# Per-head softmax weights through DRAM instead of through TensorE in an attention stage of a fused two-layer kernel

## The chip, the cores and the metric

The kernel runs on one core of a Trainium2 chip. The metric is the device time of one execution in microseconds. The time before the change is the median of 3 runs.

## The reference

Two layers work on an image of 2 x 768 x 64 x 64 in 32-bit floats, both with a group norm before and a residual behind. The first is a Mamba-like scan layer; the change does not touch it. The second, which matters here, is an attention without pairs of tokens. In short, for each batch, with 4096 tokens n, 768 channels in 12 heads h of 64 channels d:

```python
w      = (x3 @ W_qkv.T)                                   # (h, n, d)
norm   = sqrt(sum_n w*w)                                   # per channel
logits = sum_d (w / norm)**2 * temp                        # (h, n)
Pi     = softmax(logits, axis=heads)                       # (h, n)
Pi_n   = Pi / (sum_n Pi + 1e-8)
dots   = sum_n Pi_n * w**2                                 # (h, d)
out    = -(w * Pi) / (1 + dots)
out    = out @ W_out.T
```

Pi has one number for each head and token. It must be multiplied with w, which lies with channels on the partitions; so each of the 12 rows of Pi has to be copied to the 64 partitions of its head.

## The kernel before

Each batch is cut into 8 tiles of 512 tokens (`NQ`, `QL`), and the 768 channels into 6 chunks of 128 (`KM`); a chunk holds two heads. The product with W_qkv ("p1") and the product with W_out ("p3") of a tile are made of 6 products of 128 output channels each. Most of them run in `strassen`, a schedule that saves matmuls and that fills TensorE. Between these schedules lies `attention(b, ...)`, once for each batch. It makes Pi for all 8 tiles of batch b, multiplies it with w, and sums `dots`.

The order of all instructions is written out by hand (the schedule is manual); each engine, and SP's queue of loads and stores, takes its own instructions in that order. Waits between engines come from the data.

So that TensorE has something to do in `attention`, 12 ordinary products are held back for it: for batch 0 the p1 products of the first two tiles of batch 1, for batch 1 the p3 products of the last two tiles of batch 0. `product()` runs one of them; `half_a()` runs its first three matmuls and issues the loads of a product three places on, `half_b(between)` the last three, then whatever is passed as `between`, then the eviction (on ScalarE for p1, on VectorE for p3, which is stored by SP).

For one tile j the steps are:

- `squares`: ScalarE squares w, six chunks, two tiles ahead.
- `head_rows`: TensorE sums the squares over the channels of each head (pr); ScalarE copies the result (lt).
- `head_columns`: TensorE turns it so that tokens lie on partitions (pl).
- `softmax_a`: VectorE takes the maximum over the heads (mx) and subtracts it (e), ScalarE takes exp. pr and pl share one bank of PSUM.
- `softmax_b`: VectorE normalizes e, copies it four times side by side into `pi4`, and sums it into `phs`; TensorE transposes the copy (pt), ScalarE copies the result to `pit`.
- `spread`: six matmuls with a matrix of zeros and ones, `esel`, copy each row of `pit` to the 64 partitions of its head, into PSUM (ppz, ppo).
- `times_pi`: VectorE multiplies this with w into a fresh slot v; w is kept for the next step.
- `pi_sums`: VectorE multiplies v with w and sums over the tokens in one instruction, into `dots`; the slot of w is given back.

In the loop over j, step j runs `spread`, `times_pi` and `pi_sums` of tile j beside `head_rows`, `head_columns` and the softmax of tile j + 1. Ahead of the loop stand two products (one of them the argument `lead`) and the softmax of tile 0. Behind it come one product, the sum over tokens of Pi (a matmul into pp), the factor `at` = -1 / (1 + dots), the first loads and sums of the next `strassen` (`behind()`), and one more product (`more`).

Slots of 128 x 512 floats are handed out by `take()` and given back by `give()`; they are reused in the order in which they came back. `wk` is a pool of work tiles with two buffers for each tag unless a number is given.

Of the kernel before, what the change touches and what calls it, by code (L numbers as in the profile page):

```python
# [7 lines left out]
F32 = mybir.dt.float32  # L8
# [59 lines left out]
def both_layers(  # L68
    ctx, tc, nc, consts, x, in_wP, xp_wP, dt_wP, out_wT, pc_in, comb_in, pick_in, xsum_in, gavg_in, gsel_in, wo_dr, bc_dr, s_dr, x1, stats1,
    qkvP, woutP, temp_c, hcol_in, hsel_in, esel_in, out  # L70
# [583 lines left out]
    x1s, w1s, pis, pits, ats, dots, phs = {}, {}, {}, {}, {}, {}, {}  # L654
# [371 lines left out]
    def head_rows(b, j):  # L1026
# [6 lines left out]
        lt = wk.tile([P, QL], F32, tag="du", name=f"lt{b}_{j}", bufs=2)  # L1033
# [20 lines left out]
    def softmax_b(b, j):  # L1054
# [5 lines left out]
        pi = pi4[j % 2]  # L1060
        nc.vector.tensor_copy(pi[:, :, :, :HEADS], e.unsqueeze(2).to_broadcast([P, NB4, 4, HEADS]))
# [3 lines left out]
        for q in range(NB4):  # L1065
            nc.tensor.matmul(  # L1066
                pt[:, q * P : (q + 1) * P], pi[:, q, :, :].rearrange("p c h -> p (c h)"), ident, start=True, stop=True
            )
        pit = wk.tile([P, QL], F32, tag="delta", name=f"pit{b}_{j}", bufs=3)
        nc.scalar.copy(pit, pt)  # L1070
        pits[b, j] = pit

    def spread(b, j, ms):

        for m in ms:
            if m in (0, 4):
                pits["z"] = psZ.tile([P, 2, 512], F32, tag="pz", name=f"ppz{b}_{j}_{m}")
            if m == 2:
                pits["o"] = [psO.tile([P, 512], F32, tag=f"po{e}", name=f"ppo{e}_{b}_{j}") for e in range(2)]
            pb = pits["o"][m % 2] if m in (2, 3) else pits["z"][:, m % 2, :]  # L1080
            r = 32 * (m % 4)
            nc.tensor.matmul(pb, esel[r : r + HEADS, m, :], pits[b, j][r : r + HEADS, :], start=True, stop=True)  # L1082
            pits[b, j, m] = pb

    def times_pi(b, j, ms):
        for m in ms:
            w, v = w1s[b, m, j], take()
            nc.vector.tensor_mul(v, pits.pop((b, j, m)), w)
            w1s[b, m, j] = v
            pis[b, j, m] = w  # L1090

    def pi_sums(b, j, ms):
        for m in ms:
            w = pis.pop((b, j, m))
            nc.vector.tensor_tensor_reduce(w, w1s[b, m, j], w, 1.0, 0.0, ALU.mult, ALU.add, dots[b][:, m, j : j + 1])
            give(w)

    def attention(b, lead, more, behind):
# [4 lines left out]
        product(lead)  # L1103
        head_rows(b, 0)
        squares(b, 1)
        half_a()
        head_columns(b, 0)
        softmax_a(b, 0)
        half_b(lambda: softmax_b(b, 0))
        for j in range(NQ):  # L1110
            last = j + 1 == NQ
            if not last:
                head_rows(b, j + 1)
            spread(b, j, range(4))
            times_pi(b, j, range(4))
# [497 lines left out]
```

## Time and profile before

| | us |
|---|---|
| median of 3 runs | 3725.79 (3723.79 to 3728.96) |
| profiled execution | 3722.47 |
| its span, first to last instruction | 3720.7 |
| first `attention`, first product to the next Strassen schedule | 2939.2 to 3051.1 |
| second `attention` | 3385.4 to 3498.6 |
| PE busy in the span | 3532.7 (95%) |
| DVE (VectorE) busy | 2871.3 (77%) |
| ACT (ScalarE) busy | 2559.3 (69%) |
| POOL (GpSimd) busy | 1779.2 (48%) |

The mean granted clock of TensorE was 0.987. The table's shares are means over the whole span, most of which is the first layer; what the change is worth is read from the two stretches of `attention`. PE is TensorE's matmuls, PEld its loads of weights. A line of the profile names the line of the kernel, the engine, the operation and the tiles (out<-in). A matmul of 32-bit floats appears as two instructions. Where the profile lists "u" and "v", these are slots.

### The profile page before, as it was taken

The page shows a single profiled execution, that of the slowest core. Times are in us where ns is not written, and L with a number is a line of the kernel's source. Part 1 is how long each engine was busy: PE and PEld are TensorE (multiplying, and loading weights), DVE is VectorE, ACT ScalarE, POOL GpSimd, SP SyncE. Part 2 cuts the span into 40 slices and gives each one's busy share as a digit, 9 for nine tenths or more (in the row PEclk, how much of TensorE's full clock was granted, in tenths as well). Part 3 has the DMA queues.
Part 4 walks back from the last instruction along what each step waited for, and adds up shares of the span by engine and source line. Part 5 has one row for each costly group of instructions (what it writes and reads, how often), then busy time and mean ns, then how long its engine had stood idle before and what let it go on. Part 6 is the DMA issues. An engine that isn't in the chain of part 4 may idle for free. (4 is left out here: it accounts for less than half of the span.)

```text
span 3720.7 us, 37791 instructions
## 1 busy us (share of the span) xinstructions
PE 3532.7 (95%) x11088; PEld 1756.0 (47%) x11088; DVE 2871.3 (77%) x2615; ACT 2559.3 (69%) x4982; POOL 1779.2 (48%) x1813
## 2 busy tenths in 40 slices
PE   5968999999999999999899999999999999999999
PEld 3423333333333333333343333333347658886688
DVE  7899999999999999999999999997721362224522
ACT  2688889888988898889788888897633542244221
POOL 0355555555555555555555655554443313330232
PEclk9978999999999999999999999999999999999999
DMA  9877898998989999898898989897676538764487
GB/s 352 234 171 161 181 206 181 207 205 189 209 175 211 199 199 207 183 205 181 189 206 193 208 175 208 198 201 181 139 206 176 194 92 267 253 210 124 155 270 245
DMA packets 380302, 738.98 MB, mean 199 GB/s; under 512 B 44305, under 2 KB 116945, under 8 KB 376001
## 3 DMA queue, kind: packets, MB, share of 16 engines
q0 software_dynamic: 146208, 270.08, 42.8%
q1 hardware_dynamic: 233888, 466.49, 38.2%
q8 instruction: 90, 1.47, 0.2%
q14 instruction: 116, 0.94, 0.1%
HBM read 440.96 MB, written 60.03 MB: 135 GB/s over the span
## 5 line engine op out<-in xcount | busy, mean ns | idle before, releaser
L362 PE MATMUL pa<-u,w 128*128 128x512 f32 (+1 forms) x2304 | 1045.2, 604 | 31.3 <-ACT carry L377 19.5
L603 PE MATMUL po<-u,w 128*128 128x512 f32 x2256 | 1019.1, 602 | 44.8 <-DVE u L615 44.5
L539 DVE TENSOR_TENSOR_SCAN s<-da,s 128x2052 f32<-128x2052 f32 x192 | 851.1, 4433 | 19.5 <-DVE s L537 0.9
L362 PEld LDWEIGHTS pa<-u,w 128*128 128x128 f32 x2304 | 433.0, 193 | 627.8 <-issue 478.5
L603 PEld LDWEIGHTS po<-u,w 128*128 128x128 f32 x2256 | 419.6, 191 | 633.7 <-issue 540.9
L526 POOL TENSOR_TENSOR ysum<-da 128x1024 f32<-128x1024 f32 x192 | 384.7, 2004 | 583.4 <-DVE da L546 468.3
L461 DVE SCALAR_TENSOR_TENSOR acc<-xs,pc,acc 128x512 f32<-128x512 f32 x742 | 558.9, 753 | 30.5 <-ACT acc L415 12.4
L514 ACT ACTIVATE da<-dl,neg_a 128x512 f32<-128x512 f32 x768 | 489.5, 713 | 0.0
L537 DVE TENSOR_TENSOR s<-du,bc 128x2048 f32<-128x2048 f32 x192 | 438.8, 2285 | 64.1 <-POOL du L518 56.9
L433 POOL DMA_DIRECT2D tm<-tm x309 | 267.5, 866 | 446.1 <-ACT tm L427 408.9
L546 DVE TENSOR_TENSOR da<-s,bc 128x2048 f32<-128x2048 f32 x192 | 440.0, 2292 | 6.3
L533 POOL DMA_DIRECT2D u<-ysum x384 | 377.5, 1242 | 2.8 <-issue 2.3
L427 ACT ACTIVATE tm<-xs,pc 128x512 f32<-128x512 f32 x486 | 317.1, 717 | 17.2 <-DMA tm<-tm 6.2
L415 ACT ACTIVATE acc<-xs,pc 128x512 f32<-128x512 f32 x192 | 132.4, 690 | 240.7 <-DVE u L461 229.3
L518 POOL TENSOR_TENSOR du<-dl,u 128x512 f32<-128x512 f32 x192 | 243.6, 1269 | 0.0
L439 POOL DMA_DIRECT2D u<-tm x177 | 205.2, 1159 | 56.1 <-issue 45.4
L886 PE MATMUL po_p<-v,w 128*128 128x256 f32 x672 | 171.7, 379 | 1.4 <-ACT po_p L983 1.4
L886 PE MATMUL po_p<-u,w 128*128 128x256 f32 x624 | 159.7, 379 | 0.0
L461 DVE SCALAR_TENSOR_TENSOR u<-xs,pc,acc 128x512 f32<-128x512 f32 x192 | 143.6, 748 | 9.2
L831 POOL TENSOR_TENSOR v<-u 128x256 f32<-128x256 f32 x21 | 15.6, 758 | 276.9 <-ACT u L849 263.0
L886 PE MATMUL acc_p<-u,w 128*128 128x256 f32 x556 | 143.7, 382 | 4.5 <-DMA w<-woutP 3.3
L886 PE MATMUL psa_p<-u,w 128*128 128x256 f32 x554 | 141.0, 380 | 4.7 <-DMA w<-qkvP 3.6
(285 smaller groups left out, 4916.3 us busy)
## 6 DMA issues: line engine op xcount, KB each, us to landing
u<-ysum POOLq DMA_DIRECT2D x384, 256.0 KB, 5.9
tm<-tm POOLq DMA_DIRECT2D x309, 256.0 KB, 4.4
w<-in_wP SPq DMA_DIRECT2D x192, 384.0 KB, 4.7
w<-wo_dr SPq DMA_DIRECT2D x192, 384.0 KB, 5.4
u<-x SPq DMA_DIRECT2D x263, 256.0 KB, 5.1
w<-s_dr_p SPq DMA_DIRECT2D x288, 192.0 KB, 3.7
u<-tm POOLq DMA_DIRECT2D x177, 256.0 KB, 5.9
bc<-bc_dr SPq DMA_DIRECT2D x32, 1024.0 KB, 7.8
```

The lines of the kernel that those rows point to most:

```text
L362: nc.tensor.matmul(pa[:, :nn], w[:, k, :], xts[i, k][:, :nn], start=(k == 0), stop=(k == KM - 1))
L427: nc.scalar.activation(tm.rearrange("p (h w) -> p h w", w=W), xs[:, dy : dy + TR, dx : dx + W], AF.Copy, scale=pc[:, c, PC_W + j : PC_W + ...
L433: nc.gpsimd.dma_start(tms[a][0], tms[a][q], accum_op=ALU.add)
L461: nc.vector.scalar_tensor_tensor(dst, xs[:, dy : dy + TR, dx : dx + W], pc[:, c, PC_W + j : PC_W + j + 1], acc, ALU.mult, ALU.add)
L514: nc.scalar.activation(das[g % 2][:, n, 1:], deltas[g], AF.Exp, scale=neg_a[:, c, n : n + 1])
L526: nc.gpsimd.tensor_add(ysum[:, 0 : 2 + g % 2 : 1 + g % 2, :], da[:, 0:2, 1:], da[:, 2:4, 1:])
L533: nc.gpsimd.dma_start(us[g], ysums(g, n), accum_op=ALU.add)
L537: nc.vector.tensor_mul(s[:, :, 1:], dus.pop(g).unsqueeze(1).to_broadcast([P, NS, TL]), bc[:, :NS, :])
L539: nc.vector.tensor_tensor_scan(sf, das[g % 2].rearrange("p n l -> p (n l)"), sf, 0.0, ALU.mult, ALU.add)
L546: nc.vector.tensor_mul(das[g % 2][:, :, 1:], s[:, :, 1:], bc[:, NS:, :])
L603: nc.tensor.matmul(po[e], w[:, kk, e * P : (e + 1) * P], us[i * KI + k], start=(k == 0), stop=(k == KI - 1))
L886: nc.tensor.matmul(dst, half[:, k, :], tiles[blocks[seq[i][0]][:3]][what][k], start=(start and k == 0), stop=(k == KH - 1), skip_group_che ...
```

## The change

Pi is spread over the partitions by DMA. `softmax_b` transposes e itself (12 columns of weights instead of 128), and its 12 rows are stored to DRAM (`pi_dr`). `load_pi` reads them back, each row to 64 partitions, in 12 loads for a tile on SP's queue, into six buffers `pib`. There is one set of six, so the loads of a tile wait for the products with the tile before.

The products with Pi and their sums (`times_pi`, `pi_sums`) run one step of the loop later, beside the softmax of two tiles on; the products with the last two chunks now stand between `softmax_a` and `softmax_b`, ahead of the first two sums. Both inputs of `times_pi` are now in SBUF. The sum of the last chunk is made by GpSimd (the product) and ScalarE (the sum over tokens). One product fewer stands ahead of the tiles and one more behind. In the tail, the last tile's products and sums begin with the last chunk. `spread`, `esel` and `pi4` are gone.

```diff
@@ head_rows
-        lt = wk.tile([P, QL], F32, tag="du", name=f"lt{b}_{j}", bufs=2)
+        lt = wk.tile([P, QL], F32, tag="du", name=f"lt{b}_{j}")
@@ softmax_b
         nc.vector.tensor_mul(e, e, sm.unsqueeze(2).to_broadcast([P, NB4, HEADS]))
-        pi = pi4[j % 2]
-        nc.vector.tensor_copy(pi[:, :, :, :HEADS], e.unsqueeze(2).to_broadcast([P, NB4, 4, HEADS]))
         nc.vector.tensor_reduce(phs[b][:, j, :], e.rearrange("p q h -> p h q"), AX.X, ALU.add)
 
         pt = psS.tile([P, 512], F32, tag="st", name=f"pt{b}_{j}")
         for q in range(NB4):
-            nc.tensor.matmul(
-                pt[:, q * P : (q + 1) * P], pi[:, q, :, :].rearrange("p c h -> p (c h)"), ident, start=True, stop=True
-            )
-        pit = wk.tile([P, QL], F32, tag="delta", name=f"pit{b}_{j}", bufs=3)
-        nc.scalar.copy(pit, pt)
-        pits[b, j] = pit
-
-    def spread(b, j, ms):
+            nc.tensor.matmul(pt[:HEADS, q * P : (q + 1) * P], e[:, q, :], ident, start=True, stop=True)
+        pit = wk.tile([P, QL], F32, tag="du", name=f"pit{b}_{j}")
+        nc.scalar.copy(pit[:HEADS, :], pt[:HEADS, :])
+        nc.sync.dma_start(pi_dr[b][j], pit[:HEADS, :])
+
+    def load_pi(b, j, ms):
 
         for m in ms:
-            if m in (0, 4):
-                pits["z"] = psZ.tile([P, 2, 512], F32, tag="pz", name=f"ppz{b}_{j}_{m}")
-            if m == 2:
-                pits["o"] = [psO.tile([P, 512], F32, tag=f"po{e}", name=f"ppo{e}_{b}_{j}") for e in range(2)]
-            pb = pits["o"][m % 2] if m in (2, 3) else pits["z"][:, m % 2, :]
-            r = 32 * (m % 4)
-            nc.tensor.matmul(pb, esel[r : r + HEADS, m, :], pits[b, j][r : r + HEADS, :], start=True, stop=True)
-            pits[b, j, m] = pb
+            for e in range(2):
+                h = slice(e * HD, (e + 1) * HD)
+                nc.sync.dma_start(pib[m][h, :], pi_dr[b][j][2 * m + e : 2 * m + e + 1, :].partition_broadcast(HD))
@@ times_pi
-            nc.vector.tensor_mul(v, pits.pop((b, j, m)), w)
+            nc.vector.tensor_mul(v, pib[m], w)
@@ pi_sums
             w = pis.pop((b, j, m))
+            if m == KM - 1:
+                nc.gpsimd.tensor_mul(w, w1s[b, m, j], w)
+                nc.scalar.activation(w, w, AF.Copy, accum_out=dots[b][:, m, j : j + 1])
+                give(w)
+                continue
             nc.vector.tensor_tensor_reduce(w, w1s[b, m, j], w, 1.0, 0.0, ALU.mult, ALU.add, dots[b][:, m, j : j + 1])
@@ attention
-    def attention(b, lead, more, behind):
+    def attention(b, behind):
+        pib[:] = [wk.tile([P, QL], F32, tag=t, name=f"pi{t}{b}_{q}", bufs=3) for t in ("sq", "delta") for q in range(3)]
         ...
         head_weights(b)
-        product(lead)
+        half_a()
         head_rows(b, 0)
         squares(b, 1)
-        half_a()
+        half_b()
         head_columns(b, 0)
         softmax_a(b, 0)
-        half_b(lambda: softmax_b(b, 0))
+        head_rows(b, 1)
+        softmax_b(b, 0)
+        load_pi(b, 0, range(KM))
+
         for j in range(NQ):
-            last = j + 1 == NQ
-            if not last:
+            if 0 < j < NQ - 1:
                 head_rows(b, j + 1)
-            spread(b, j, range(4))
-            times_pi(b, j, range(4))
+            if j:
+                times_pi(b, j - 1, range(4))
             if j + 2 < NQ:
                 squares(b, j + 2)
             half_a()
-            if not last:
+            if j:
+                load_pi(b, j, range(4))
+            if j + 1 < NQ:
                 head_columns(b, j + 1)
                 softmax_a(b, j + 1)
-            spread(b, j, (4, 5))
-            pi_sums(b, j, range(2))
-            half_b(lambda: last or softmax_b(b, j + 1))
-            times_pi(b, j, (4, 5))
-            pi_sums(b, j, range(2, KM))
+            if j:
+                times_pi(b, j - 1, (4, 5))
+                load_pi(b, j, (4, 5))
+                pi_sums(b, j - 1, range(2))
+            half_b(lambda: j + 1 == NQ or softmax_b(b, j + 1))
+            if j:
+                pi_sums(b, j - 1, range(2, KM))
+        half_a()
+        times_pi(b, NQ - 1, (KM - 1, *range(KM - 1)))
+        pi_sums(b, NQ - 1, (KM - 1, *range(KM - 1)))
+        half_b()
+        product()
 
         ph = gp1.tile([P, HEADS], F32, name=f"phs{b}")
         nc.vector.tensor_reduce(ph, phs[b].rearrange("p j h -> p h j"), AX.X, ALU.add)
-        product()
         pp = psS.tile([P, 512], F32, tag="st", name=f"pp{b}")
         ...
         behind()
-        product(more)
+        product()
@@ the constants
-        esel = gp1.tile([P, KM, P], F32, name="esel")
-        nc.sync.dma_start(esel, esel_in)
-        pi4 = [gp1.tile([P, NB4, 4, 32], F32, name=f"pi4_{j}") for j in range(2)]
-        for pi in pi4:
-            nc.gpsimd.memset(pi, 0.0)
```

More of the change, by code (lines that the diff above doesn't have):

```diff
@@ L69, in both_layers @@
     ctx, tc, nc, consts, x, in_wP, xp_wP, dt_wP, out_wT, pc_in, comb_in, pick_in, xsum_in, gavg_in, gsel_in, wo_dr, bc_dr, s_dr, x1, stats1,
-    qkvP, woutP, temp_c, hcol_in, hsel_in, esel_in, out
+    qkvP, woutP, temp_c, hcol_in, hsel_in, pi_dr, out
 ):
@@ L653, in both_layers @@
         nc.gpsimd.memset(t, 0.0)
-    x1s, w1s, pis, pits, ats, dots, phs = {}, {}, {}, {}, {}, {}, {}
+    x1s, w1s, pis, pits, ats, dots, phs, pib = {}, {}, {}, {}, {}, {}, {}, []
     def gn_next(b):
@@ L1469, in both_layers @@
         )
-        attention(0, 1, 1, prepare)
+        attention(0, prepare)
         for j in rest:
@@ L1475, in both_layers @@
         prepare, products = strassen([("p3", 1, j) for j in range(NQ)])
-        attention(1, 1, 1, prepare)
+        attention(1, prepare)
         products()
@@ L1481, in mamba_then_attention @@
 def mamba_then_attention(
-    ctx, tc, x, in_wP, xp_wP, dt_wP, out_wT, pc_in, comb_in, pick_in, xsum_in, qkvP, woutP, temp_c, ident_in, gavg_in, gsel_in, hcol_in, hsel_in, esel_in, out
+    ctx, tc, x, in_wP, xp_wP, dt_wP, out_wT, pc_in, comb_in, pick_in, xsum_in, qkvP, woutP, temp_c, ident_in, gavg_in, gsel_in, hcol_in, hsel_in, out
 ):
@@ L1503, in mamba_then_attention @@
     s_dr = {k: dram.tile([KM // 2, 4, P, KM // 2, P], F32, name=f"s_dr_{k}") for k in ("p1", "p3")}
+    pi_dr = [[dram.tile([HEADS, QL], F32, name=f"pi_dr{b}_{j}") for j in range(NQ)] for b in range(NB)]
     both_layers(
         tc, nc, consts, x, in_wP, xp_wP, dt_wP, out_wT, pc_in, comb_in, pick_in, xsum_in, gavg_in, gsel_in, wo_dr, bc_dr, s_dr, x1, stats1,
-        qkvP, woutP, temp_c, hcol_in, hsel_in, esel_in, [out[b].rearrange("c h w -> c (h w)") for b in range(NB)],
+        qkvP, woutP, temp_c, hcol_in, hsel_in, pi_dr, [out[b].rearrange("c h w -> c (h w)") for b in range(NB)],
     )
@@ L1557 @@
     hsel[32 * (hd // 2 % 4) + hd, hd] = 1.0
-    esel = np.zeros((P, DM), np.float32)
-    for r in range(0, P, 32):
-        esel[r + ch // HD, ch] = 1.0
     def by_chunk(w):
@@ L1599 @@
         "hsel_in": hsel,
-        "esel_in": esel.reshape(P, KM, P),
     }
```

## The prediction, made before the result was known

> **What bounds the kernel now.** I read the slices and the chain of the page first (PE is busy nine tenths nearly throughout, and the chain that ended last runs along PE), then the waits, timelines and busy times of the two stretches that `attention` fills, 2939.2 to 3051.1 us and 3385.4 to 3498.6 us. Busy times by stretch, for one tile of the loop over `j` in each (span, then busy time of PE, PEld, DVE, ACT, POOL; clock; DMA share; GB/s):
>
> ```profile
> core 0: us, PE busy (x) PEld busy (x) DVE busy (x) ACT busy (x) POOL busy (x), PEclk, DMA share, GB/s
> 2966.90:2978.10 11.20, 11.20 (x58) 5.22 (x56) 8.66 (x25) 6.21 (x14) 0.00 (x0) 1.00 0.20 58
> 3401.50:3412.70 11.20, 11.20 (x58) 5.21 (x56) 7.70 (x21) 4.53 (x9) 0.00 (x0) 1.00 0.25 83
> ```
>
> PE has no gap, POOL does nothing, DMA works 2.2 to 2.9 us of a tile. So a tile lasts as long as its matmuls. Timeline of PE for that tile (start, us):
>
> ```profile
> 2964.03 1.05 PE L1066 MATMUL pt<-ident,pi 128*128 128x128 f32 x8
> 2965.02 1.48 PE L1031 MATMUL pr<-u,gcol 128*32 128x512 f32 x9
> ...
> 2966.86 0.70 PE L1082 MATMUL ppz<-pit,esel 12*128 12x512 f32 x2
> ...
> 2967.93 2.84 PE L692 MATMUL mmp<-v,w 128*128 128x512 f32 x6
> 2970.61 0.96 PE L1042 MATMUL pl<-hsel,lt 128*128 128x12 f32 x8
> 2971.50 1.13 PE L1082 MATMUL ppz<-pit,esel 12*128 12x512 f32 x4
> 2972.55 1.13 PE L692 MATMUL mmp<-v,w 128*128 128x512 f32 x2
> ```
>
> From start to start, with the next pt at 2975.23: pt 0.99, pr 1.84, spread 1.07, half_a 2.68, pl 0.89, spread 1.05, half_b 2.68; sum 11.20. The two spreads, 2.12 us, go away. What is late next is the softmax between pl and the next pt, on DVE:
>
> ```profile
> 2971.60 0.21 DVE L1048 TENSOR_REDUCE mx<-pl 128x4 f32<-128x48 f32 x1 [1.08 <-PE pl L1042]
> 2971.84 0.21 DVE L1050 TENSOR_TENSOR e<-pl,mx 128x48 f32<-128x48 f32 x1
> 2971.97 0.68 DVE L1095 CUSTOM_DVE_ANT_0 u<-u,u 128x512 f32<-128x512 f32 x1
> ...
> 2972.58 0.68 DVE L1095 CUSTOM_DVE_ANT_0 u<-v,u 128x512 f32<-128x512 f32 x1
> ...
> 2973.63 0.21 DVE L1059 TENSOR_TENSOR e<-e,sm 128x48 f32<-128x48 f32 x1
> ```
>
> Two sums (0.61 each) stand between the subtraction and the rest of the softmax; e is ready at 2973.84, 3.23 us after pl began. PE reaches pt 4.62 us after pl began, so it doesn't wait.
>
> **The loop after.** Between the subtraction and the rest of the softmax now stand two products with Pi (0.60 each by the pitch of L1088) and the two sums: e is ready at 3.23 + 1.20 = 4.43, and PE starts pt 0.06 later (2952.67 to 2952.73, the first tile), at 4.49. Without spread PE is there at 0.81 (pl to a product, 2948.98 to 2949.79) + 2.68 = 3.49, so it now waits 1.00. The loop closes over this chain: 4.49 + pt 0.99 + pr 1.84 + half_a 2.68 = **10.00 us**, not the 9.08 that the matmuls alone would give. The smaller pt (12 columns of weights) is costed at nothing: its moving side stays 128 columns, and at most 0.1 is in it.
>
> The product that moves to GpSimd comes on top. It starts when the second product with Pi is done, in the middle of this chain, and lasts 1.26 us (L518, 128x512). DVE's sums, and now its products with Pi, read two tensors of SBUF. The trace has such DVE instructions beside GpSimd's in two places (a line's min/median/max ns; then a timeline):
>
> ```profile
> L287 DVE TENSOR_TENSOR wg<-wg,wmean x4: 939/944/6882, 151.6 to 171.7; 128x768 f32<-128x768 f32 x4
> ```
>
> ```profile
> 1784.75 1.26 POOL L518 TENSOR_TENSOR du<-dl,u 128x512 f32<-128x512 f32 x1
> 1784.84 1.19 DVE L662 TENSOR_TENSOR msq<-mv,stats 128x6 f32<-128x6 f32 x1
> ```
>
> L662's work is 0.17 us (as L663's after it), but it ended with GpSimd's instruction; one L287 lasted 6.88 us, through three of GpSimd's. Reductions and reciprocals, which read one tensor, kept their 0.19 and 0.18 beside GpSimd. So the chain grows. Lower end 0.81: GpSimd gets in only at the softmax's reduction and reciprocal and hides 0.45 there. Upper end 1.26: it gets in between the two sums. I take 1.10, near the upper end, because in both rows the waiting side was held till GpSimd had ended; it isn't the full 1.26 because a GpSimd instruction that met a running DVE one (172.24) grew by 0.32 where 0.44 overlapped. A tile: **11.10 us**, 0.10 less than now; twelve such tiles (j = 1 to 6, twice): **-1.2**.
>
> On the same point the Trainium skill, page "SBUF — State Buffer", section "SBUF: two separate sides", says that whichever starts first keeps the shared ports for its whole instruction. In the L287 row DVE had started 0.40 us before GpSimd and yet came last, so row and rule differ on who wins. By the rule DVE's back-to-back sums would keep GpSimd out until the softmax, the lower end, and the sum would be 3.5 lower.
>
> What the rest of the change costs in a tile lies beside this. DVE: six products 3.6, five sums 3.05, softmax 1.6, eviction 0.6 (second attention), held up 1.1: 10.0 of 11.1, and idle for over 1 us before each pl. ACT: 6.2 now, plus the sum of one chunk (0.5 and 0.2 for its accumulator): 6.9. It stands before the copy lt, which then ends some 3.5 us after pt; PE needs it 4.5 after.
>
> The way through DRAM: copy of pt 0.6, store landing some 2.0 us later (the load of comb, 128 KB, landed in 2.2), then 12 loads of 128 KB on SP's queue. I take 0.45 us for each: a packet of 2 KB costs one of 16 engines 97 ns on this queue, 174 on the other (share times 16 spans, over packets):
>
> ```profile
> q0 software_dynamic: 146208, 270.08, 42.8%
> q1 hardware_dynamic: 233888, 466.49, 38.2%
> ```
>
> 64 packets over 16 engines are 0.39 or 0.70; SP issues two loads in a row 0.47 apart. So 0.39 to 0.70, and 0.45 by the nearer row. The last load lands 0.6 + 2.1 + 5.4 + 2.0 = 10.1 after pt; the first product of that tile starts on DVE 12 us after, the last some 17. So the loads are hidden in the loop, and so are the waits that they bring to SP. Behind them SP has the next store and a product's weights, wanted three products later. DMA: 5.4 + 2.2 to 2.9 of 11.1.
>
> The Trainium skill, same page, section "Door 1: The DMA port swizzle", speaks against these loads: 64 partitions reach half the ports, measured there at 196 GB/s. No row here shows it. An estimate by it is 0.67 us a load; the loop would still hide them, the ends below would grow by 2.6 each, and the sum would be +0.9.
>
> **Ahead of the tiles.** First attention now: 2939.22 to the third pr at 2965.02, 25.8 us. After: half_a 2.6, pr 1.85, half_b 2.65, pl 0.85. The next pr uses pl's bank and waits 0.6. Exp waits on ACT behind six squares (3.1), an eviction with its norm (1.8) and the table load (1.28), so e comes at 2951.4 and pt ends at 2952.4; then 2.7, 0.85, 2.65, 1.0: 2959.6. That is 20.4, and 5.15 for the product moved behind: 25.6, so **-0.1** with rounding. Second attention: no table load and no eviction on ACT; 18.5 + 5.15 against 25.4 (3385.39 to 3410.81): **-1.8**.
>
> **Behind the tiles.** Count from e of the last tile. PE: pt till 1.05, three products 15.45: 16.5. DVE: the earlier tiles till 9.8 (with two evictions 11.0); the last Pi lands at 1.65 + 2.15 + 5.4 + 2.0 = 11.2; then six products 3.6, held up 1.1, five sums 3.05, reduction 0.3: 19.25, in the second attention with two more evictions 20.45. PE waits 2.75 and 3.95 for pp. From pp to Strassen 5.4, the wait for weights at 3498 (1.1) gone, since the stores are issued before pp. Less the moved product: 15.45 + 2.75 + 5.4 - 5.15 = 18.4 against 18.8 (3032.28 to 3051.06): **-0.4**; 19.65 against 20.55: **-0.9**.
>
> **Sum:** -1.2 - 0.1 - 1.8 - 0.4 - 0.9 = -4.4. The profiled execution took 3722.47 us (span 3720.7), 3.3 below the median 3725.79: 3718.1 there, 3721 as a median. With GpSimd's ends (0.81, 1.26) and the loads' (0.39, 0.70) the sum goes from -9 to +4.
>
> **Rivals.** *GpSimd costs DVE nothing*, because it gets its turn in DVE's gaps: for it, DVE is idle over a tenth of a tile; against it, the two rows. Tiles of 10.00, and 1.1 less at each end: -14.4 - 1.9 - 3.5 = -19.8, 3706. *The loads become the bound* (slower): SP's 12 loads and the other transfers (2.2, 2.9) no longer fit a tile. It decides from 0.69 to 0.75 us a load. For it: the one broadcast load of the kernel, bc, 1 MB, landed in 7.8 us, 0.98 for 128 KB. Against it: that time includes some 2 us of fixed latency and other queues' traffic. At 0.85 the tiles last 12.4 and 13.1: 6 x (1.2 + 1.9) = 18.6, the ends 9.6 more: +25, 3751; at 0.98 3773. *GpSimd is kept out until DVE is idle*, and the sum on ACT holds lt back: tiles of 11.9, +8 in the loop, about 3731.
>
> **Chances.** Forecast 0.48, cheap GpSimd 0.36, loads 0.13, late sum 0.03. About 0.2%, 7.5 us, is what a measurement of this kernel can tell from no change. Faster: 0.36 and 0.03 of the forecast's lower edge, 0.39; slower: the loads and a little of the others, 0.15; same 0.46. Range 3704 to 3735: from the cheap GpSimd to the ends with slow loads; the loads as bound are left out. The forecast's own range is 3717 to 3730.
>
> **What would show it.** Loop period (pr to pr) near 11.1, with PE waiting 2 us at pt for e; a DVE sum or e's product stretched by about 1 us beside L1095's GpSimd instruction; waits of 3 to 4 us at pp. A period of 10.0 would make GpSimd's cost wrong; waits of DVE for Pi's loads inside the loop would make the loads' price wrong.

## The result and the profile after

The changed kernel took 3740.20 us (median of 4 runs, 3735.65 to 3745.11) where the kernel before took 3724.79 on the same chip (median of 4): a ratio of 1.0042, with a 95% interval of 1.0030 to 1.0055. It is slower by 15.4 us; 3721 was forecast. The profiled execution took 3735.65 us with a span of 3733.9, that is 13.2 more than the span before.

The two stretches that `attention` fills hold all of it. The first went from 111.84 to 120.26 us (2938.20 to 3058.46), the second from 113.23 to 120.36 (3391.01 to 3511.37): +15.6 together. The rest of the program is 2.4 shorter. What TensorE waits for in the two stretches after (engine, line and tile waiting, then who released it; us in total, number of times, longest):

```profile
PE pt L1064 <- DVE e L1059: 11.2, 6, 1.9
PE pp L1139 <- DVE phs L1137: 5.5, 1, 5.5
PE pl L1042 <- ACT lt L1034: 4.2, 1, 4.2
...
PE pt L1064 <- DVE e L1059: 12.1, 6, 2.4
PE pp L1139 <- DVE phs L1137: 8.0, 1, 8.0
```

The first three lines are the first attention, the last two the second. The wait of 1.9 us in each tile was forecast (TensorE at pt, for e). The waits at pp are twice the 2.75 and 3.95 of the forecast, and the wait of 4.2 at pl was not in it at all.

**One tile.** Busy times of one tile of the first attention, and of two tiles of the second (span, then busy time of PE, PEld, DVE, ACT, POOL; clock; DMA share; GB/s):

```profile
2985.07:2995.99 10.92, 9.00 (x40) 4.43 (x41) 8.87 (x23) 6.70 (x15) 1.58 (x1) 1.00 0.54 170
3409.41:3421.17 11.76, 9.40 (x43) 4.61 (x42) 8.28 (x19) 4.53 (x9) 1.55 (x1) 0.96 0.75 245
3421.17:3433.50 12.33, 10.29 (x42) 4.92 (x42) 9.35 (x23) 5.16 (x11) 1.59 (x1) 0.90 0.79 226
```

TensorE now has 9.0 us of work in 10.92, so two spreads are gone and a wait has taken nine tenths of their place. In the second attention three of six tiles are longer (11.4, 12.7, 12.6 from pt to pt) and the granted clock is not full. At the end of the first of these, ScalarE's exponential stands behind a square that waits 3.83 us for a slot, which an output store has to give back; that store had gone out on SP's queue (3414.20) only behind Pi's first twelve loads. TensorE then waits 2.36 us at pt instead of 1.92:

```profile
3418.60 0.63 ACT L1009 ACTIVATE u<-u 128x512 f32<-128x512 f32 x1 [3.83 <-DMA out<-u]
...
3420.11 1.48 PE L1064 MATMUL pt<-ident,e 128*12 128x128 f32 x7 [2.36 <-DVE e L1059]
...
3432.83 0.94 PE L1064 MATMUL pt<-ident,e 128*12 128x128 f32 x7 [2.04 <-DVE e L1059]
```

The other two each hold a stretch of 3.4 us at half the granted clock, 3420.25 to 3423.66 (0.51) and 3434.0 to 3437.4 (0.50), right behind the waits of 2.36 and 2.04 us; that is worth some 1.7 us in each, and they are 1.80 and 1.65 longer than 10.92. So the clock, and not a longer chain, makes most of the three tiles' extra length.

The timeline of VectorE (start, us) in the first attention's tile, and GpSimd's one instruction in it:

```profile
2991.68 0.21 DVE L1050 TENSOR_TENSOR e<-pl,mx 128x48 f32<-128x48 f32 x1
2991.80 1.28 DVE L1079 TENSOR_TENSOR u<-pidelta,u 128x512 f32<-128x512 f32 x2
2993.00 0.69 DVE L1091 CUSTOM_DVE_ANT_0 u<-v,u 128x512 f32<-128x512 f32 x1
...
2993.61 1.75 DVE L1091 CUSTOM_DVE_ANT_0 u<-v,u 128x512 f32<-128x512 f32 x1
...
2993.23 1.58 POOL L1087 TENSOR_TENSOR u<-u,u 128x512 f32<-128x512 f32 x1 [9.34 <-DVE u L1079]
```

The second sum takes 1.75 us instead of 0.68, because GpSimd's product got in between two sums that stand back to back. That is 1.07 of hold-up in the softmax's chain.

**The first step.** SP, then ScalarE, then TensorE, in the first attention (the brackets give the idle time before an instruction and what ended it):

```profile
2953.92 3.71 SPq L1074 DMA_DIRECT2D pisq<-pi_dr  x6
2957.68 3.92 SPq L1074 DMA_DIRECT2D pidelta<-pi_dr  x6
2961.69 0.53 SPq L686 DMA_DIRECT2D w<-qkvP  x1
2962.32 0.38 SPq L677 DMA_DIRECT2D u<-x  x1
...
2966.27 0.81 ACT L680 ACTIVATE u<-u,bias,scale 128x512 f32<-128x512 f32 x1 [5.66 <-DMA u<-x]
2966.99 0.56 ACT L1034 COPY lt<-pr 128x512 f32<-128x512 f32 x1
...
2967.60 1.67 PE L1042 MATMUL pl<-hsel,lt 128*128 128x12 f32 x7 [4.25 <-ACT lt L1034]
```

The twelve loads of the first Pi stand on SP's queue ahead of the loads that step 0's product issues. One of those is an x1 chunk of a later product (L677). It goes out at 2962.32, ScalarE's norm of it (L680) waits for it, and the copy lt, which TensorE needs at once for pl, stands behind that norm.

**The end.** SP, VectorE and TensorE behind the last tile of the first attention; its e was ready at 3028.70:

```profile
3030.49 0.32 SPq L1067 DMA_DIRECT2D pi_dr<-pit  x1
3030.91 0.34 SPq L686 DMA_DIRECT2D w<-qkvP  x1
3032.07 3.65 SPq L1074 DMA_DIRECT2D pisq<-pi_dr  x6
3035.77 3.78 SPq L1074 DMA_DIRECT2D pidelta<-pi_dr  x6
...
3042.76 0.69 DVE L1079 TENSOR_TENSOR v<-pidelta,v 128x512 f32<-128x512 f32 x1 [4.21 <-DMA pidelta<-pi_dr]
...
3050.96 0.57 PE L1139 MATMUL pp<-phs,ones 128*128 128x12 f32 x2 [5.51 <-DVE phs L1137]
3051.38 3.76 PE L692 MATMUL mmp<-u,w 128*128 128x512 f32 x4
3054.93 1.12 PE L692 MATMUL mmp<-v,w 128*128 128x512 f32 x2
```

Twelve loads take SP 7.5 us, 0.62 each from start to start. The last Pi lands 14.05 us after e, VectorE has been idle for 4.2, and pp comes 5.5 late. Behind pp four matmul instructions take 3.76 us where six took 2.74 before the wait: the granted clock is 0.50 from 3048.29 to 3055.12. The product behind pp takes 7.1 us in place of 5.2, in the second attention 8.1.

### The profile page after: what moved, and what is told of

Its sections match the earlier page's. It is cut to its first block, busy times and chain, and to the rows that moved or that the text cites. A ratio compares the mean times of both kernels' runs of the same rounds, so it can differ in the third digit from the quotient of the medians.

```text
span 3733.9 us, 37812 instructions
## 1 busy us (share of the span) xinstructions
PE 3505.8 (94%) x10896; PEld 1745.7 (47%) x10896; DVE 2876.1 (77%) x2567; ACT 2569.0 (69%) x5014; POOL 1806.3 (48%) x1827
## 5 line engine op out<-in xcount | busy, mean ns | idle before, releaser
L886 PE MATMUL po_p<-u,w 128*128 128x256 f32 x666 | 167.2, 379 | 0.0
L886 PE MATMUL po_p<-v,w 128*128 128x256 f32 x630 | 160.7, 379 | 1.5 <-ACT po_p L983 1.4
L375 ACT COPY xs<-pa 128x512 f32<-128x512 f32 (+1 forms) x192 | 109.9, 572 | 41.9 <-PE pa L362 37.8
L530 ACT ACTIVATE u<-u,pc 128x512 f32<-128x512 f32 x192 | 136.7, 712 | 2.1 <-POOL du L518 2.1
```

Source lines behind the costliest of these rows:

```text
L886: nc.tensor.matmul(dst, half[:, k, :], tiles[blocks[seq[i][0]][:3]][what][k], start=(start and k == 0), stop=(k == KH - 1), skip_group_che ...
```

## The experiments

The theory behind the first runs was W, waits: the loop is held by the softmax chain with GpSimd's hold-up in it, and the loss comes of waits at the ends, which SP's slow issues make, and of the half clock behind them. The rivals were L (the loads on SP hold the loop as well), P (the bytes of the transfers set the pace, not the issues) and C (the clock falls with the load, whatever the waits). Since runs of one kernel spread by 0.3%, the table gives beside the ratio to the kernel before on the same chip (95% interval; its medians were 3724.1 to 3725.5) the sum of the two attention stretches in the one profiled execution. The rest of the program, which is the same in all of them, took 3493 to 3508 us there, and the profiled executions of h1 and g4 lie 8 and 10 us above their medians.

| kernel | us | ratio to before | both stretches, us |
|---|---|---|---|
| before | 3724.79 | 1 | 225.1 |
| the changed kernel | 3740.20 | 1.0042 (1.0030 to 1.0055) | 240.6 |
| e1_dve_sum | 3737.13 | 1.0028 (1.0018 to 1.0039) | 238.3 |
| e2_x1_first | 3731.88 | 1.0017 (1.0008 to 1.0027) | 232.9 |
| e3_tail_in_order | 3740.34 | 1.0038 (1.0026 to 1.0050) | 239.6 |
| e4_two_queues | 3737.13 | 1.0033 (1.0021 to 1.0045) | 238.0 |
| f1_merged_loads | 4126.36 | 1.1077 (1.1062 to 1.1092) | 628.5 |
| f2_tail_in_order | 3730.33 | 1.0015 (1.0007 to 1.0024) | 229.3 |
| f3_combined | 4109.87 | 1.1033 (1.1018 to 1.1048) | 612.0 |
| f4_fill | 3740.57 | 1.0038 (1.0026 to 1.0051) | 241.7 |
| g1_copies | 3748.57 | 1.0061 (1.0049 to 1.0073) | 251.3 |
| g2_combined | 3714.39 | 0.9969 (0.9957 to 0.9981) | 216.7 |
| g3_two_issuers | 3744.16 | 1.0049 (1.0036 to 1.0062) | 243.2 |
| g4_combined_12_loads | 3719.66 | 0.9986 (0.9977 to 0.9994) | 220.2 |
| h1_squares_later | 3739.78 | 1.0035 (1.0021 to 1.0049) | 244.8 |
| h4_first_loads_only | 3727.31 | 1.0002 (0.9993 to 1.0011) | 227.4 |
| h2_copies_early_total | 3714.76 | 0.9968 (0.9956 to 0.9979) | 211.9 |
| h3_early_total | 3717.43 | 0.9979 (0.9970 to 0.9988) | 216.0 |

**GpSimd's sum (e1_dve_sum).** In `pi_sums`:

```diff
-            if m == KM - 1:
-                nc.gpsimd.tensor_mul(w, w1s[b, m, j], w)
-                nc.scalar.activation(w, w, AF.Copy, accum_out=dots[b][:, m, j : j + 1])
-                give(w)
-                continue
```

> The sixth chunk's sum goes back to DVE; everything else as in the changed kernel. Theory W (the loop is held by the softmax chain, in which GpSimd's product holds a DVE sum up by 1.06 us a tile; the loss comes from waits at the ends): the sum of 1.74 us returns to 0.68, the loop's period falls from 10.92 to 9.9-10.0, twelve tiles give -11 to -12, the two tails about -0.5 each (the stretched product back to 0.69, one sum of 0.61 more): 3727 to 3729. Rival L (the loads on SP, 12 of 0.6 us a tile, or their traffic hold the loop): the period stays at 10.9 and the time at 3739 to 3741.

The loop did what W says: in the first attention five tiles went from 10.92 to 9.86 us. But the total fell by 3 us only, which is within the intervals, and not by the 11 to 13 that W expected. What the tiles gained came back behind them, and SP shows how. The last tile's e was ready at 3024.74:

```profile
3024.59 3.78 SPq L1074 DMA_DIRECT2D pidelta<-pi_dr  x6
3028.47 0.50 SPq L1067 DMA_DIRECT2D pi_dr<-pit  x1
3029.07 0.34 SPq L686 DMA_DIRECT2D w<-qkvP  x1
3031.34 3.65 SPq L1074 DMA_DIRECT2D pisq<-pi_dr  x6
3035.04 3.78 SPq L1074 DMA_DIRECT2D pidelta<-pi_dr  x6
```

The store of the last Pi waits 3.7 us after e until SP has issued the tile before's loads (in the changed kernel 1.8, which is the copy). SP's round is store, weights, the store's landing, twelve loads: 10.5 us, longer than the 9.86 of the tile. A tile does not notice, since Pi is wanted a tile later; but SP falls behind by 0.6 us a tile, and pp waits 7.6 us instead of 5.5 (12.0 instead of 8.0 in the second attention). Theory L was half right: SP's round does not set the tile's length here, but a tile below 10.5 us is paid for at the end.

**The first step's order (e2_x1_first).** `load_pi(b, 0, ...)` moved behind step 0's `half_a()`:

```diff
-        load_pi(b, 0, range(KM))
...
             half_a()
-            if j:
-                load_pi(b, j, range(4))
+            load_pi(b, j, range(4) if j else range(KM))
```

> Only the place of the first tile's Pi loads on SP's queue: behind the loads of the product of step 0 instead of ahead of them. Theory W: the x1 load is issued some 7 us earlier, lt no longer stands behind a norm that waits for it, the 4.2 us wait of TensorE at pl in the first attention goes, and with it the 6.8 us at half clock behind it: -4 to -7, 3733 to 3736; the second attention, which loads no x1, is unchanged. Rival (the wait only moves: the first products with Pi now wait for their loads): no change, 3739 to 3741.

The wait at pl is gone, and the tile behind it takes 10.98 us in place of 16.33. The two stretches are 7.7 us shorter and the median 8.3. It is the cheapest half of the loss: no work changed, only the place of twelve loads in a queue.

**The end.** Three attempts. e3_tail_in_order was flawed: it loaded the sixth chunk of the last tile before the product that still needed the tile before, so that product took the later Pi and waited for its landing.

```diff
+            order = (KM - 1, *range(KM - 1)) if j + 1 == NQ else range(KM)
-                load_pi(b, j, range(4))
+                load_pi(b, j, order[:4])
...
+        for m in order:
+            times_pi(b, NQ - 1, (m,))
+            pi_sums(b, NQ - 1, (m,))
```

> Last tile only: the sixth chunk's Pi is loaded first instead of last, and DVE takes each chunk's product and sum as the chunk lands. Twelve loads as before, landing as late as before. Theory W: after the last landing (14 us after e) DVE has one product, one sum and the reduction left, 1.5 us, so pp waits 0 to 0.5 us instead of 5.5 and 8.0, the half clock behind these waits goes too (the product behind pp takes 5.2 instead of 7.1 and 8.1): -5.3 -1.9 and -7.7 -2.9, in all -14 to -18, 3722 to 3726. Rival C (the half clock comes of the stretch's load, not of the wait): the product behind pp still takes 7 to 8, -13, 3727. Rival L (traffic of the loads): waits of the same size at other places, 3736 to 3741.

No gain: the waits at pp fell to 3.6 and 3.2 us, but in the loop's last step VectorE now waited for what it no longer waited for behind the loop, and in the second attention a product of TensorE's waited 3.8 us for it. The second form keeps the loads as they are:

```diff
-        half_a()
-        times_pi(b, NQ - 1, (KM - 1, *range(KM - 1)))
-        pi_sums(b, NQ - 1, (KM - 1, *range(KM - 1)))
-        half_b()
-        product()
-
-        ph = ...
+        product()
+        half_a()
+        for m in range(KM):
+            times_pi(b, NQ - 1, (m,))
+            pi_sums(b, NQ - 1, (m,))
+        ph = ...
+        half_b()
```

> The last tile again, with its loads left as they are (in e3_tail_in_order the sixth chunk's load of the last tile had been put ahead of the product that still needed the tile before, so this product took the later tile's Pi and waited for it). DVE does the two products' evictions that are due first, then product and sum chunk by chunk in the order of landing. Theory W: the first Pi lands 7.2 us after e, then one each 1.2 us, as fast as DVE takes them; after the last (14) one product is left and the total is ready before TensorE comes to pp at 16.5: no wait at pp (5.5 and 8.0 before), the product behind it in 5.2 (7.1, 8.1): -5.5 -1.9 -8.0 -2.9 = -18 at most, 3721 to 3726. Rival (the half clock comes of the stretch's load and not of the wait): the product behind pp still takes 7 to 8 us, 3726 to 3729.

The two stretches are 11.3 us shorter, the median 9.9. In the first attention pp waits 0.8 us and from pp to Strassen it is 5.45 instead of 7.5. In the second, pp still waits 3.2 and the product behind it still runs at half clock: there VectorE reaches the last tile only behind an eviction, and a product and its sum take it 1.34 us a chunk, since the sum waits for the product. The third attempt lets ScalarE issue half of the last tile's loads:

```diff
-                nc.sync.dma_start(pib[m][h, :], ...)
+                eng = nc.scalar if e and j == NQ - 1 else nc.sync
+                eng.dma_start(pib[m][h, :], ...)
```

> Last tile only: of the twelve Pi loads every second one is issued by ACT instead of SP. Theory W (an issue on SP of 0.62 us for each load sets the last landing): the last lands 3.5 us earlier, some 10.5 us after e instead of 14; pp waits 2 and 4.5 us instead of 5.5 and 8.0; with part of the half clock gone -7 to -11 in all, 3729 to 3733. Rival (the 64-partition transfers themselves pass no faster than one in 0.6 us, whoever issues them): the last lands 14 us after e as now, time 3739 to 3741.

From the first issue to the end of the last it took 5.3 us for twelve loads instead of 7.5, and the two waits at pp fell from 13.5 to 7.4 in total. The first six loads went out in 2.0 us from the two queues, the last six in 3.4 with gaps, whose cause was not followed up; the transfer engines were busy at a share of 0.87 meanwhile. The last Pi landed 8.5 us after the first issue instead of 10.7. In the median it is 3 us, in the two stretches 2.6; the second attention's tiles were longer in this run (12.2, 12.6, 11.7, 12.6), which took back part of the gain.

**Fewer, larger loads.** One load a chunk, first with a source of two rows:

```diff
-            for e in range(2):
-                h = slice(e * HD, (e + 1) * HD)
-                nc.sync.dma_start(pib[m][h, :], pi_dr[b][j][2 * m + e : 2 * m + e + 1, :].partition_broadcast(HD))
+            rows = pi_dr[b][j][2 * m : 2 * m + 2, :].unsqueeze(1).to_broadcast([2, HD, QL])
+            nc.sync.dma_start(pib[m], rows)
```

> One load of 128 partitions and 256 KB per chunk of Pi in place of two of 64 partitions and 128 KB: 6 issues a tile instead of 12, the same bytes. Theory W (SP's 0.6 us for each issue sets when the last Pi lands): 6 x 0.6 = 3.7 us instead of 7.5; the last Pi lands some 10.4 us after e instead of 14; pp waits 2 and 4.4 us instead of 5.5 and 8; the x1 load of the first step stands behind 3.7 us of issues instead of 7.5, so the wait of 4.2 at pl falls under 1; with some of the half clock 3726 to 3731. Rival P (the bytes set it: the transfers pass at 128 KB in 0.6 us, and an issue of 256 KB then takes SP 1.2): no change, 3738 to 3742.

Neither theory: 386 us slower, tiles of 35 us. Two stretches of it while Pi's loads run (columns as above):

```profile
3000.00:3018.00 18.00, 10.16 (x42) 4.59 (x40) 5.20 (x14) 6.81 (x15) 0.00 (x0) 0.88 0.13 49
3028.00:3034.00 6.00, 2.95 (x16) 1.73 (x18) 4.99 (x15) 0.99 (x3) 1.64 (x1) 0.50 0.12 45
```

The DMA share is 0.12 to 0.13: 2 of 16 transfer engines (0.125) carry the load, at 45 to 49 GB/s. The Trainium skill, page "DMA: Bandwidth & Descriptors", section "Rules for kernel authors", says that an outermost dimension of fewer than 16 entries confines a transfer to at most so many engines; the outermost dimension here is 2, and the runs agree. So f3_combined, which rests on these loads (its edits are those of g2_combined below with this form), told nothing on its question:

> All in one: the sixth sum on DVE, the first tile's Pi loads behind step 0's product loads, one load per chunk, the tail in order, and the tile before's sums all behind the softmax, so that between subtraction and exponential's sum only two products with Pi stand. Theory W: the chain from pl to e falls from 4.9 (with the hold-up) to 3.4 us, TensorE no longer waits for it; the tile is then 9.1 (matmuls alone) to 9.6 (DVE: six products 3.6, six sums 3.7, softmax 1.6, eviction 0.6) instead of 11.2 before: twelve tiles -19 to -25, the ends -2 to -6, against before; no half clock between the attentions' first and last tiles: 3695 to 3705. Rival L (the way through DRAM or its traffic holds the loop once the chain does not): tiles of 10.5 or more, 3712 and above.

Its tiles were 34 to 36 us. With a source of 16 rows, for which the store writes each row eight times:

```diff
-        nc.sync.dma_start(pi_dr[b][j], pit[:HEADS, :])
+        nc.sync.dma_start(pi_dr[b][j], pit[:HEADS, :].unsqueeze(1).to_broadcast([HEADS, 8, QL]))
...
+            rows = pi_dr[b][j][2 * m : 2 * m + 2].rearrange("e c q -> (e c) q")
+            nc.sync.dma_start(pib[m], rows.unsqueeze(1).to_broadcast([16, 8, QL]))
```

> One load per chunk again, but in a form that all transfer engines share: the store writes each row of Pi eight times to DRAM, and a load's source is 16 rows, each read for 8 partitions (in f1_merged_loads the source was 2 rows read for 64 partitions each, and two packets at a time were under way). Everything else as in the changed kernel. Theory L (SP's round of one tile, store, three other issues, the store's landing and 7.5 us of Pi loads, is 10.5 to 10.9 us and so holds the second attention's tiles, and sets the last landing): 6 issues in place of 12 make the round 7 to 8 us; DVE no longer waits for Pi in the second attention (tiles of 11.4 to 12.7 return to 10.9), the wait at pl in the first step falls from 4.2 under 1, the last Pi lands 2 to 3 us earlier: 3722 to 3730. Rival P (the transfers of 128 KB in 0.6 us are the limit, not the issues): an issue of 256 KB takes SP 1.2, 3738 to 3742.

SP's issues came out as L says:

```profile
2955.18 0.91 SPq L1067 DMA_DIRECT2D pi_dr<-pit  x1
2959.85 1.88 SPq L1073 DMA_DIRECT2D pisq<-pi_dr  x3
2961.78 1.87 SPq L1073 DMA_DIRECT2D pidelta<-pi_dr  x3
```

A load of 256 KB takes SP 0.64 us from start to start, where one of 128 KB took 0.62: SP pays by the load and not by the byte, and P's 1.2 us did not come. But the transfers are close behind the issues. Behind the last issue for the first attention's last tile all transfer engines are busy (columns as above):

```profile
3044.20:3049.72 5.52, 5.52 (x14) 2.45 (x13) 0.00 (x1) 0.00 (x0) 0.00 (x0) 1.00 1.04 263
```

At 263 GB/s 128 KB take 0.50 us. The last Pi landed 5.5 us after the last issue instead of 3.2, and 9.3 after the first instead of 10.7: half the issues were 3.7 us shorter, the landing only 1.4 earlier. So P is right in part: the bytes leave room for some 0.1 us a load below SP's 0.62. And the store, with eight copies, holds the loads up for 4.7 us in the first step where the plain one held them up for 1.6; the waits for it take back what the issues give: the wait at pl grew to 6.0, and the kernel is 8 us slower than the changed one. With GpSimd as a second issuer instead:

```diff
+                eng = nc.gpsimd if e else nc.sync
-                nc.sync.dma_start(pib[m][h, :], ...)
+                eng.dma_start(pib[m][h, :], ...)
```

> The two loads of a chunk as in the changed kernel, but every second one issued by GpSimd, which has only one product a tile to do: SP 6 issues, GpSimd 6 of about 1 us each. Theory L: SP's round falls to 7 to 8 us as in g1_copies, the first step's x1 load is issued 3.7 us earlier, the last Pi lands some 3 us earlier: 3724 to 3732. Rival P (the transfers set it): 3738 to 3742; and if GpSimd's issues hold its product or DVE up, slower than that.

The wait at pl fell to 3.0 and the waits at pp to 8.2 in total, but most tiles rose to 11.3 to 13.0 us: GpSimd's issues stand ahead of its product, which can hold up VectorE's second sum (2.13 us in one tile instead of 1.75). The first attention's last Pi landed 8.9 us after the first of its loads instead of 10.7, with the transfer engines at a share of 0.91. L's number was missed: the landing came 1.8 us earlier and not 3, and the tiles grew.

**The loads left out (h4_first_loads_only).**

```diff
-        for m in ms:
+        for m in ms if j == 0 else ():
```

> As the changed kernel, but only the first tile's Pi is loaded; the other tiles are multiplied with it, so 84 of the 96 loads of each attention are left out; stores, products and sums are all there. The first attention's wait at pl stays (its loads are the first tile's). Theory L (loads): the second attention's tiles at 10.9 (-4), no wait at pp beyond what DVE's own work gives (2 to 3 us instead of 5.5 and 8, as in the prediction with the last Pi landing in time), and less half clock: -10 to -16 in all, 3724 to 3730. Theory B (buffers alone): the second attention's tiles stay above 11, 3728 to 3733.

The two stretches are 13.2 us shorter and the median 12.9. Four of the second attention's tiles are 10.92 (three in the changed kernel); the first two, beside the loads that stay, are 11.9 and 12.3, so these six are only 1.5 shorter together and not the 4 that L expected. The ends gain more, some 15 us: pp waits 1.2 and 1.9, and the product behind it runs at full clock in both:

```profile
3497.08 0.36 PE L1139 MATMUL pp<-phs,ones 128*128 128x12 f32 x2 [1.91 <-DVE phs L1137]
3497.30 1.10 PE L723 MATMUL mmp<-u,w 128*128 128x512 f32 x2
3498.24 1.02 PE L723 MATMUL mmp<-v,w 128*128 128x512 f32 x2
3499.10 2.74 PE L723 MATMUL mmp<-u,w 128*128 128x512 f32 x6
3501.67 1.02 PE L723 MATMUL mmp<-v,w 128*128 128x512 f32 x2
```

So the loads of tiles 1 to 7 cost 13 us; the place of the first tile's on the queue, by e2, cost 8. The two were not run together. Leaving the loads out takes away their issues and their bytes at once, so this run does not tell the two apart.

**The squares (h1_squares_later).** ScalarE's `squares(b, j + 2)` moved from ahead of `half_a()` to behind `softmax_a(b, j + 1)`.

> As the changed kernel, but ScalarE's six squares of the tile after next are queued behind the exponential of the next tile's softmax instead of ahead of it. Theory B (in the second attention the squares wait 1.4 to 3.8 us for buffers that the output stores and DVE's late products free, and the exponential stands behind them): the second attention's tiles go from 11.4 to 12.7 to 10.9, -3 to -5: 3735 to 3737. Theory L (the loads hold these tiles): they stay at 11.4 to 12.7, 3739 to 3741.

No change of the median. The tiles of the second attention were 10.9 to 12.6 as before, so the squares' place alone does not make them long. The first is now 10.92; in the second, two products with Pi wait 0.23 and 0.55 us for loads ahead of the sums, TensorE's wait at pt grows to 2.89, and half clock follows. With the squares ahead it was the output store's slot that came late; both the stores and Pi's loads stand on SP's queue. In the changed kernel SP's round there, from one store of Pi to the next, is:

```profile
3425.58 0.50 SPq L1067 DMA_DIRECT2D pi_dr<-pit  x1
3426.17 0.35 SPq L713 DMA_DIRECT2D out<-v  x1
3426.61 0.38 SPq L709 DMA_DIRECT2D v<-x  x1
3427.04 0.45 SPq L686 DMA_DIRECT2D w<-woutP  x1
3428.58 3.65 SPq L1074 DMA_DIRECT2D pisq<-pi_dr  x6
3432.33 3.90 SPq L1074 DMA_DIRECT2D pidelta<-pi_dr  x6
3436.33 0.50 SPq L1067 DMA_DIRECT2D pi_dr<-pit  x1
```

10.75 us, and the next is 11.0 (3447.33): SP has no room left in a tile of 10.92.

**The clock (f4_fill).** Matmuls with no reader, ahead of pt and pp:

```diff
+    def fill(n, name):
+        z = psZ.tile([P, 2, 512], F32, tag="pz", name=f"fill{name}")
+        for _ in range(n):
+            nc.tensor.matmul(z[:, 0, :P], ident, ident, start=True, stop=True)
...
+        if j > 1:
+            fill(6, f"{b}_{j}")
...
+        fill((18, 27)[b], f"{b}")
```

> Only added work: TensorE gets matmuls whose result nobody reads, 6 of 128 columns (some 1.3 us) ahead of pt from the third tile on and 18 and 27 (some 4 and 6 us) ahead of pp, where it waits now. Nothing else is changed, and the waits' ends stay where they are. Theory H (in the runs so far each 3.41 us step in which TensorE stood idle for over about 1.92 us was followed by a step at half the granted clock): no such step is left at these places; the second attention's tiles of 11.4 to 12.7 us return to 10.9 (-4 to -5) and the product behind pp to 5.2 (-1.9, -2.9): 3730 to 3735, faster although only work is added. Rival C (the clock falls with the load, whatever the waits): as many steps at half clock or more, 3740 to 3745.

The total is as it was, but the two ends tell the theories apart. In the first, the fill left 1.35 us of wait, and the product behind pp came at full clock:

```profile
3057.73 0.36 PE L1147 MATMUL pp<-phs,ones 128*128 128x12 f32 x2 [1.35 <-DVE phs L1144]
3057.95 1.96 PE L692 MATMUL mmp<-u,w 128*128 128x512 f32 x4
...
3511.75 0.57 PE L1147 MATMUL pp<-phs,ones 128*128 128x12 f32 x2 [3.41 <-DVE phs L1144]
3512.16 2.05 PE L723 MATMUL mmp<-u,w 128*128 128x512 f32 x2
```

In the second the fill was too short, 3.41 us of wait were left, and there two matmul instructions take 2.05 us, half the speed. The clock follows the wait, not the load. But H's tiles did not come: two of the second attention's stayed long (12.9, 12.5). In the one of 12.9, at full clock, products with Pi waited for loads (four waits, 1.9 us together) and the exponential came 0.90 us late for VectorE, behind squares that waited 5.38 us for an output store's slot; the fill left 2.58 us of wait there, and the tile of 12.5 began at half clock. So delays from SP's queue lengthen a tile there by themselves too. Counted over 16 of the profiles (without f1 and f3), both stretches, in steps of 3.41 us on the grid of the clock's records: of 62 steps at full clock in which TensorE stood idle for 2.0 us or more in all, all 62 were followed by a step at half clock; of 39 with 1.9 to 2.0 us, 4; of 851 with less, 2. The loop's wait of 1.92 us lies just at this edge.

**All together.** g2_combined: e1's and e2's and f2's edits, g1's loads, and all sums of the tile before behind the softmax, so that only two products with Pi stand in the chain:

```diff
                 load_pi(b, j, (4, 5))
-                pi_sums(b, j - 1, range(2))
             half_b(lambda: j + 1 == NQ or softmax_b(b, j + 1))
             if j:
-                pi_sums(b, j - 1, range(2, KM))
+                pi_sums(b, j - 1, range(KM))
```

> f3_combined with the loads of g1_copies: sixth sum on DVE, first loads behind step 0's, one load per chunk over all transfer engines, tail in order, sums of the tile before behind the softmax. With SP's round at 7 to 8 us and the chain at 3.4 from pl to e, TensorE or DVE holds a tile: 9.1 to 9.6 us instead of 11.2 before; 12 tiles -19 to -25, the ends 0 to -5: 3697 to 3706. If the loads still hold it: tiles of 10.5 or more, 3712 and above.

It is faster than the kernel before, 0.9969 (0.9957 to 0.9981), 11 us. In the first attention the tiles are 8.9 to 10.1 us, nearly as expected; in the second 9.1 to 12.9, so that the time stayed 8 us above the expected range. There VectorE's products with Pi wait for loads and for slots that the output stores give back; which of the two holds the tiles is left open. With the twelve loads:

> g2_combined with the changed kernel's twelve loads of 64 partitions. Theory L: the chain is out of the way, so SP's round of 10.5 us (first attention) and 10.9 (second) now is what a tile lasts, 1 us or more above g2_combined's: 3710 to 3718. Rival (the loads never held the loop, only the chain did): the tiles of g2_combined, 9.1 to 9.6, and a time within 4 us of its.

3719.66: the first attention's tiles start at 8.9 and rise to 9.8 to 10.8 as SP falls behind, which is L's sign; but in the second six tiles take 64.0 us together against g2's 66.8, and the gap to g2 is 5.3 us, just outside the rival's 4 and with overlapping intervals. Neither is shown. Last, the total of Pi (phs, pp and its reciprocal) behind the first of the last products, and the squares behind the exponential:

```diff
+        ph = ...
         product()
+        pp = ...
+        rp = ...
         half_a()
         for m in range(KM):
             times_pi(b, NQ - 1, (m,))
             pi_sums(b, NQ - 1, (m,))
-        ph = ...
         half_b()
-        pp = ...
-        rp = ...
```

> g2_combined with two orders changed: the squares behind the exponential, and the total of Pi (phs, pp and its reciprocal) taken after the first of the last products, since it needs only the softmaxes and not the last tile's sums. No work added or taken. Expected: no wait at pp (4.3 and 4.7 us there), the product behind it at once and at full clock; then Strassen waits for the sums, 1.0 of small DVE operations and ScalarE's scaling, some 2 to 4 us shorter than pp's way in each attention; the second attention's tiles from 11.2 on average to 9.5 if the squares held them: -6 to -15 against g2_combined, 3700 to 3708. If loads hold them: tiles stay at 11, -4 to -8, 3706 to 3710.

> h2_copies_early_total with the changed kernel's twelve loads of 64 partitions and plain stores. By theory L SP's round of 10.5 us (first attention) and 10.9 (second) holds the tiles, so only the end gains: -4 to -8 against g4_combined_12_loads, 3712 to 3716. By theory B the second attention's tiles fall to 9.5: 3704 to 3709.

The two stretches are 4.8 and 4.2 us shorter than g2's and g4's in the profiled executions, but the medians differ by +0.4 and -2.2, and both miss their ranges. The waits at pp fell to 1.1 and 1.2 us in h2 (2.3 and 3.7 in h3), but in its second attention the next Strassen schedule then waited 3.97 us for a load of weights. So the order of the end gains less than expected, at most 2 us that these runs can show.

## Why the prediction was wrong, by its own steps

- **The loop** was right: 10.92 us against a forecast of 11.10. GpSimd's hold-up was 1.07 against 1.10, and without it the tile was 9.86 against 10.00.
- **The prefixes** were right: 20.3 and 18.4 us to the third pr against 20.4 and 18.5.
- **"So the loads are hidden in the loop, and so are the waits that they bring to SP"** is the step that failed, in three places. First, it named a product's weights as what stands behind the loads, and did not go through what else `half_a` issues: the x1 chunk, whose norm ScalarE does ahead of lt. Tile 1 took 16.33 us instead of 11.10, +5.2; e2 removed it. Second, it compared the loads with the room on the transfer engines (5.4 + 2.2 to 2.9 of 11.1) and not with SP's round, in which the store, its landing and three other issues are in line with them: 10.75 to 11.0 us in the second attention. Three tiles there were longer by 3.4 together against the forecast: the first because an output store behind Pi's loads gave its slot back late, the other two mostly by a step at half clock behind waits of over 2 us, which such delays had brought about. h4, without the loads of tiles 1 to 7, brought only the third of them back to 10.92. Third, "It decides from 0.69 to 0.75 us a load" was for that reason too high a bound: at the measured 0.62 SP's round was full.
- **The price of a load**, 0.45 us, was mis-sized: 0.62, which is within the bounds of 0.39 to 0.70. It came from the time of the packets; the loads are paced by SP's issues, which cost nearly the same for 256 KB (0.64), with the transfers close behind (0.50 us for 128 KB in g1). The landing was 3.2 us after the last issue instead of 2.0. Together the last Pi came 14.05 us after e and not 11.2, and pp waited 5.5 and 8.0 instead of 2.75 and 3.95: +6.8.
- **TensorE's clock** was taken as full. From pp to Strassen it took 2.1 and 3.2 us more than the forecast's 5.4, beside the two steps in the tiles above. f4 and the count above show why: waits of 2 us or more in a step of 3.41 us cost half speed in the next. A wait is dearer than its length.
- The sum of these against the forecast: +5.2 + 3.4 + 6.8 + 5.3, less 1.4 for the other eight tiles (10.92 instead of 11.10), is +19.3. The two stretches were forecast at 220.7 (225.1 less 4.4) and took 240.6, so 0.6 is not accounted for.
- The rival *the loads become the bound* had the right sign and the right queue, at a smaller size and mostly at the ends. *GpSimd costs DVE nothing* is wrong by the trace; *GpSimd is kept out until DVE is idle* too.
- **The two rules of the Trainium skill.** Of the rule on the shared ports (page "SBUF — State Buffer", section "SBUF: two separate sides"), the trace shows both sides: GpSimd's product, recorded from 2993.23 on, took 0.32 more than its 1.26 while the first sum ran, and then the second sum waited for all of it. So each held for its one instruction, but the conclusion drawn from it, that sums back to back keep GpSimd out, was wrong: it gets in between two of them. The 0.67 us that the prediction worked out from the same page's section on the port swizzle was nearer to 0.62 than the forecast's 0.45; but g1's loads to all partitions took SP 0.64 for twice the bytes, so the agreement does not show that the ports set it.

## What to carry to other kernels

When transfers are put on a queue, go through everything behind them on that queue, instruction by instruction, up to who waits for it, and add up the queue's whole round with the landings that it waits for; room on the transfer engines does not tell whether the queue has room. Where a step is moved one tile later, its waits don't vanish but collect behind the last tile: count the way from the last result to its last use there, and take chunks in the order in which they land. A wait of the matmul engine has two prices, its length and, here from some 2 us on, the half clock behind it.

## What was not expected of the hardware

- A step of 3.41 us with 2.0 us or more of idle TensorE was followed by one at half clock in 62 of 62 cases; below 1.9 us in 2 of 851. The Trainium skill, page "TensorE: Matmul & The Clock Gate", section "What's actually happening", speaks of an idle window of about 3.4 us; here 2.0 of the 3.41 were enough.
- A load that reads rows of DRAM for many partitions each cost SP 0.62 us with 128 KB and 0.64 with 256 KB; loads of weights in the same program go out 0.47 apart.
- Behind such loads the transfer engines were full at 263 GB/s, 0.50 us for 128 KB: with half the issues the last Pi landed 1.4 us earlier and not 3.7.
- A load whose source has an outermost dimension of two used two transfer engines: 45 to 49 GB/s, a DMA share of 0.12 to 0.13.
- A store of 12 rows with eight copies each held the loads that read it up for 4.7 us in the first step, where one copy held them up for 1.6.
